# Routed experts in four sets of widths, one chosen on the chip, and two other edits to the second phase

## The chip, the cores and the metric

The kernel runs on one core of one Trainium2 chip. The metric is the device time of one execution in microseconds (us). The core has five engines that work side by side, each with its own queue of instructions which it takes in order: TensorE (PE; its weight loads are listed as PEld), VectorE (DVE), ScalarE (ACT), GpSimd (POOL) and SyncE (SP), which here issues most of the DMA transfers. An engine whose next instruction waits for another engine's result, or for a transfer, lets everything behind it in its queue wait too. "L272" means line 272 of the kernel's source.

## The reference

There are 8192 tokens of 512 numbers. They are normalised (`xn`) and go two ways: through a recurrent layer (`s`), and through a feed-forward part made of one shared expert for all tokens and 32 routed experts, of which each token takes the one with its largest gate logit (`g`). The end is `x + s * silu(g)`.

```python
scores = jax.nn.sigmoid(topk_val)[:, None]
xs = x * scores
tokens_per_expert = jnp.zeros((E,), jnp.int32).at[topk_ids].add(1)
order = jnp.argsort(topk_ids)
sorted_x = xs[order]
g = _grouped_mm(sorted_x, routed_gate_w, tokens_per_expert)
u = _grouped_mm(sorted_x, routed_up_w, tokens_per_expert)
d = _grouped_mm(jax.nn.silu(g) * u, routed_down_w, tokens_per_expert)
...
x = x + s * g
```

The gate and up weights of a routed expert are 512 by 1024 and the down weights 1024 by 512, all in fp32, so an expert brings 6 MB of weights. How many tokens an expert gets depends on the data. With the inputs of the reference, the counts, worked out from its own gate and sorted, are 343, 331, 311, 306, 306, 301, 298, 274, 272, 270, 266, 265, 265, 263, 258, 251, 250, 243, 243, 242, 237, 234, 233, 231, 228, 224, 222, 218, 217, 202, 197, 191.

## The kernel before

**Phase one** is dense. It runs over 16 chunks of 512 tokens; a written-out order of slots, 140 to a chunk (`SC`), says at which slot which step is issued (`at(slot, step)`, main loop L1429). TensorE does the input projections in `plain` and `multiply` (L701 to L802) and, as a filler between them, the output projections in `project_out` (L1030 to L1084). A unit of `project_out` is half a chunk's output: seven products P1, P2, P6, P5, P7, P3, P4 of 16 matmuls each (the line of the matmul is L1055), accumulated in two PSUM banks, `chain` and `side`. P2, P5 and P3 share `side`, so P5 cannot begin before VectorE has taken P2's result out of it (L1067: `o[0] = ps + part["a1"]`). The weights of a product come from DRAM into one of the tiles `wP`, or `far` for some of the last ones, loaded ahead by SP (L985, L988).

**The dispatch** (class `Dispatch`, L1086 to L1341) turns the gate's choices into a table: it counts the tokens of each expert, sorts the experts by count (`places`, L1156), gives the k-th largest the k-th entry of the constant list `WIDTHS`, works out each token's place (`slots`, L1240), enters the tokens into a table in DRAM by 64 scattered DMAs on POOL (`enter`, L1301), and reads it back as `idx` (`ids`, L1329). For the gathers a second form is wanted, `fours`: `numbers` (L1332) issues eight DMAs from POOL that bring the table into SBUF in two halves, and three slots later VectorE converts each half (L1338):

```python
at(now + 3, lambda: nc.vector.tensor_scalar(
    pools["fours"][:, 2 * half : 2 * half + 2, :], f, float(NA), piece[:, 0:1],
```

These steps are issued in the slots behind the last chunk, amid the last unit of `project_out`.

**Phase two** runs over the 32 experts, largest first (L1495 to L1523). Each is a `Chunk` (L170 to L363) of a fixed number of columns W, its entry of `WIDTHS` (376 down to 224, 8832 in sum); columns beyond its tokens are empty work. In `compute` (L253), eight steps j each do 4 matmuls into `e_g`, 4 into `e_u` (both L272) and, one step late, 4 into the four PSUM tiles `acc` (L261). A program matmul appears as two MATMUL records in the trace, since the numbers are fp32, so an expert is 192 records of width W. ACT (L277) and DVE (L279, L280) make `e_h` of `e_g` and `e_u`. The other steps hang between the eight: the transposes of the next expert's tokens (DVE, L248) at steps 5 to 7, the gathers of the tokens of the expert after next (POOL, L213) at step 2, the gather of the rest of the rows (POOL, L223) at step 6, the loads of the weights two experts ahead (SP, L193) at steps 1 and 7, and the finish of the expert before (DVE, ACT, and a scatter to the output on POOL, L360). Seven weight slots lie in the pools `wa` (four) and `wb` (three), each slot a tile of its own. The gathered tokens have `2 * CT` buffers (CT is 3), the rest rows `CT + 2`.

**Behind phase two** a loop (L1528 to L1556) would take experts whose count exceeds their width: it reads the number of such chunks, `nov`, into a register on each engine (L1529). With these inputs it runs zero times.

Of the kernel before, what the change touches and what calls it, by code (L numbers as in the profile page):

```python
# [17 lines left out]
P = 128  # L18
# [5 lines left out]
CT = C // P  # L24

WIDTHS = (
    376, 352, 336, 320, 320, 312, 304, 296, 296, 296, 288, 280, 280, 280, 272, 272,
    272, 264, 264, 264, 256, 256, 248, 248, 248, 240, 240, 240, 232, 232, 224, 224,
)
EPS = 1e-5  # L30


@with_exitstack
def tile_kernel(
# [14 lines left out]
    rdown_w: bass.AP,  # L49
    out: bass.AP,  # L50
):

# [27 lines left out]
    nc = tc.nc  # L80
# [20 lines left out]
    const = ctx.enter_context(tc.tile_pool(name="const", bufs=1))  # L101
# [6 lines left out]
    def work(name):  # L108
        return pools["work"].tile([P, 512], FP, tag="w", name=name)

    pools = {}
# [4 lines left out]
    ones = const.tile([P, P], FP, name="ones")  # L116
# [22 lines left out]
    iot = iota("iot", NIO, 1, 0)  # L139
    thr = iota("thr", KOV, C, 0)  # L140
    descp = iota("descp", 1, 0, E, -1)
    wid = const.tile([P, E], FP, name="wid")

    def widths(first, last):
        for e in range(first, last):
            nc.vector.memset(wid[:, e : e + 1], float(WIDTHS[e]))

    tok = iota("tok", NTILE, P, 0, cm=1)
    mhalf = const.tile([P, NT], FP, name="mhalf")
# [9 lines left out]
    ovexp = const.tile([P, MAXOV], I32, name="ovexp")  # L159
    nov = const.tile([P, 1], I32, name="nov")  # L160
    eid = const.tile([P, E], I32, name="eid")

    def expert(where):
        e = nc.values_load(
            where, engines=[ET.SP], min_val=0, max_val=E - 1,
            skip_runtime_bounds_check_because="the numbers of experts, or a count of them, clamped",
        )
        return [w[bass.ds(e, 1)].rearrange("o a b -> (o a) b") for w in (rgate_w, rup_w, rdown_w)]

    class Chunk:  # L170
# [133 lines left out]
        def store(self):  # L304

            nb = -(-self.width // BL)
            self.y = ydram[next(yturn) % len(ydram)]
            rows = self.y.rearrange("(b c) (a d) -> a c b d", c=BL, a=NA)
            for a in range(NA):
                nc.sync.dma_start(  # L310
                    out=rows[a, :, :nb, :],
                    in_=self.yT[a * BL : (a + 1) * BL, :nb].rearrange("p b m r -> p b (m r)"),
                )
# [51 lines left out]

    accs = []
    ydram = [dram.tile([C, H], FP, name=f"ydram{q}") for q in range(3)]
    yturn = iter(range(E))
    NW = 7
    turn = iter(range(3 * E))  # L370

    def alloc_w(shape, name):
        i = next(turn) % NW
        return pools["wa" if i < 4 else "wb"].tile(shape, FP, tag=f"w{i}", name=name)

    def alloc2(shape, tag, name):
        bufs = {"xs": 2 * CT, "xsT": 2, "sig": 2, "h": 3, "y": 3, "s": 2, "yT": 2, "rest": CT + 2}
        pool = pools["in" if tag in ("xs", "xsT") else "by"]
        return pool.tile(shape, FP, tag=tag, name=name, bufs=bufs[tag])

    chunks = [
        Chunk(
            alloc2, alloc_w, f"e{e}",
            lambda t, e=e: pools["idx"][:, e * CT + t : e * CT + t + 1],
            lambda t, b, e=e: pools["fours"][:, b, e * CT + t : e * CT + t + 1],
            WIDTHS[e], lambda e=e: expert(eid[0:1, e : e + 1]), e == 0, e == E - 1,
        )
        for e in range(E)
    ]

# [43 lines left out]
    class Prep:  # L434
# [127 lines left out]
        def plan(self, g):  # L562

            g += 50 if self.c == 1 else 0
            for t in range(NT):
                at(g + 2 + 2 * t, self.load, t)
                at(g + 16 + 2 * t, self.stats, t)
                at(g + 32 + 2 * t, self.normal, t)
                at(g + 35 + 2 * t, self.store, t)
                at(g + 43 + 2 * t, self.pieces, t)  # L570
                at(g + 50 + 2 * t, self.turn, t)
                late = 70 if self.c == NCHUNK - 1 else 0
                at(g + 72 + late + 2 * t, self.again, t)
# [512 lines left out]
    class Dispatch:  # L1086
# [69 lines left out]
        def places(self):  # L1156
# [26 lines left out]
            yield  # L1183
            at_pos = row("at_pos")
            nc.vector.tensor_scalar(at_pos, iot[:E, :E], pos[:, 0:1], None, ALU.is_equal)
            nc.vector.tensor_tensor(gt, at_pos, wid[:E, :], ALU.mult)
            we = total(gt, "we")
            rest = col("left")
            nc.vector.tensor_tensor(rest, cnt, we, ALU.subtract)
            ov = row("ov", KOV)  # L1190
# [141 lines left out]
        def numbers(self, half):  # L1332

            f = self.big([P, 2, NCOL], f"number{half}")
            rows = self.table.rearrange("(b c) q -> c b q", c=BL)[:, 2 * half : 2 * half + 2, :]
            for a in range(NA):
                nc.gpsimd.dma_start(out=f[a * BL : (a + 1) * BL, :, :], in_=rows)
            at(now + 3, lambda: nc.vector.tensor_scalar(  # L1338
                pools["fours"][:, 2 * half : 2 * half + 2, :], f, float(NA), piece[:, 0:1],
                ALU.mult, ALU.add,  # L1340
            ))  # L1341
# [50 lines left out]
    def table():  # L1392
        for part in (d.ranks(NCHUNK // GC - 1), d.places(), d.slots()):
            yield from part
        first = now + 3
        end = first + (21 * NTILE) // 10
        for i in range(NTILE):
            at(first + (21 * i) // 10, d.enter, i)
        at(end + 4, d.collect)
        for which in range(4):  # L1400
            at(end + 13 + which, d.merge, which)
        end = max(end + 17, END + 1)
        at(end, d.ids)
        at(end + 1, chunks[0].gather_in)
        for half in range(2):
            at(end + 2, d.numbers, half)
# [22 lines left out]
    for now in range(END):  # L1429
# [15 lines left out]
    pools["idx"] = ix.tile([P, NCOL], I32, name="idx")  # L1445
    pools["fours"] = ix.tile([P, NA, NCOL], I32, name="fours")
    c2 = ExitStack()
    pools["wa"] = c2.enter_context(
        tc.tile_pool(name="wa", bufs=1, side="right", reuse_waits="tile")
    )  # L1450
    pools["in"] = c2.enter_context(
        tc.tile_pool(name="in2", bufs=2, side="right", reuse_waits="tile")
    )
    ps_w = ctx.enter_context(
        tc.tile_pool(name="ps_w", bufs=4, space=PSUM, side="right", reuse_waits="tile")
    )
# [4 lines left out]
    k = 0  # L1461
# [29 lines left out]
    with ExitStack() as c3:  # L1491
        pools["wb"] = c3.enter_context(tc.tile_pool(name="wb", bufs=1, reuse_waits="tile"))
        pools["by"] = c3.enter_context(tc.tile_pool(name="by", bufs=2, reuse_waits="tile"))
        chunks[1].gather_in()
        for e, chunk in enumerate(chunks):  # L1495
            between = {j: [] for j in range(NI)}
            if e:
                before = chunks[e - 1]
                between[0].append(before.store)
                between[1].append(before.fetch)  # L1500
                for t in range(CT):
                    between[1 + t].append(lambda t=t: before.bias(t))
                    between[3 + t].append(lambda t=t: before.sums(t))
                    between[4 + t].append(lambda t=t: before.finish(t))
            if e == 0:
                for j, tag in enumerate("gud"):
                    between[j].append(lambda tag=tag: chunks[1].weight(tag))
            if e + 2 < E:
                between[3 if e == 0 else 1].append(lambda: chunks[e + 2].weight("g"))
                between[2].append(chunks[e + 2].gather_in)  # L1510
            if e + 1 < E:
                for t in range(CT):
                    between[5 + t].append(lambda t=t: chunks[e + 1].transpose(t))
            between[6].append(chunk.gather_rest)
            if e + 2 < E:
                between[7] += [lambda q=q: chunks[e + 2].weight(q) for q in "ud"]
            if e == E - 1:
                for t in range(CT):
                    between[7].append(lambda t=t: chunk.bias(t))
            chunk.compute(between)  # L1520
        for t in range(CT):
            for step in (chunks[-1].sums, chunks[-1].finish):
                step(t)  # L1523
    order.close()
    c2.close()

# [62 lines left out]
```

## Time and profile before

| | us |
|---|---|
| median of three runs | 4239.5 (4238.96 to 4239.67) |
| the profiled execution | 4237.99 |
| its span | 4236.3 |
| TensorE busy | 4198.9 (99% of the span) |
| weight loads busy | 3527.2 (83%) |
| VectorE / ScalarE / GpSimd busy | 2083.9 / 1978.0 / 1105.3 |
| granted clock of TensorE | 0.997 |

The span is the time from the first to the last recorded instruction; the execution's own time is 1.7 us longer, and the median of the runs is 1.5 us above the profiled one. Matmuls are pipelined: successive records overlap, and the distance from one start to the next, not the listed duration of one, is what a matmul costs on the path. In the chain of waits (the work that ended last, followed back to what released each step) the pieces are given by that distance. Idle time of an engine that isn't the bottleneck costs nothing.

### The profile page before, as it was taken

The numbers are of one execution on the slowest core, as the hardware profiler recorded it, in microseconds if no ns is written. First come the engines' busy times: TensorE is split into PE (matmuls) and PEld (weight loads), VectorE is DVE, ScalarE is ACT, GpSimd is POOL, SyncE is SP. The second block draws the span as 40 slices with busy tenths as digits, with TensorE's granted clock in tenths as the row PEclk, the third lists the DMA queues.
The fourth block names the chain that finished last, engine by engine and source line by source line (L and its number), as shares of the span: only waits on it lengthen the run. The fifth ranks groups of instructions, "written<-read, shape, count | busy, mean of one in ns | idle before, by whom it ended". The sixth has DMA issues, their size and how long they took to land.

```text
span 4236.3 us, 51931 instructions
## 1 busy us (share of the span) xinstructions
PE 4198.9 (99%) x18719; PEld 3527.2 (83%) x18719; DVE 2083.9 (49%) x3425; ACT 1978.0 (47%) x3577; POOL 1105.3 (26%) x1182
## 2 busy tenths in 40 slices
PE   9999999999999999999999999999999999999998
PEld 4688888888888888888888888866777788889998
DVE  5555555544554545555545456424444444544444
ACT  5676676666666766666767666501111111111110
POOL 3222122111221121212211225442232333323221
PEclk9999999999999999999999999999999999999999
DMA  8767666666676666766666656575666567677773
GB/s 277 244 214 231 207 216 216 210 223 206 213 226 216 217 213 203 231 202 216 222 210 220 214 177 205 179 267 181 211 227 226 205 236 242 222 253 242 243 263 113
DMA packets 506854, 925.61 MB, mean 218 GB/s; under 512 B 38397, under 2 KB 324509, under 8 KB 498402
## 3 DMA queue, kind: packets, MB, share of 16 engines
q1 hardware_dynamic: 478754, 831.89, 59.2%
q0 software_dynamic: 27840, 90.36, 6.4%
q8 instruction: 150, 2.46, 0.2%
q14 instruction: 110, 0.90, 0.1%
HBM read 805.27 MB, written 134.92 MB: 222 GB/s over the span
## 4 chain that ended last, share of the span: by engine, by line
PE 97%; DVE 1%; DMA 1%; issue 0%; ACT 0%; POOL 0%; SPq 0%; POOLq 0%; ACTq 0%
PE b L759 24%; PE u L1055 18%; PE c L759 12%; PE e_u L272 11%; PE e_g L272 11%; PE acc L261 11%; PE a L759 6%; PE b L710 3%; PE lgp L520 0%; DMA e_xs<-rec,idx 0%; PE lgt L530 0%; PE b L725 0%; DMA x<-in_L_attn_x_dram 0%; DMA e_rest<-rec,idx 0%; POOL s L1007 0%
## 5 line engine op out<-in xcount | busy, mean ns | idle before, releaser
L759 PE MATMUL b<-t,sums 128*128 128x256 f32 x2400 | 616.1, 379 | 1.2 <-DVE t L681 1.2
L1055 PE MATMUL u<-wP,s 128*128 128x256 f32 x2032 | 598.4, 380 | 6.1 <-issue 6.1
L277 ACT ACTIVATE e_sig<-e_g 128x280 f32<-128x280 f32 (+15 forms) x256 | 101.8, 398 | 931.8 <-PE e_g L272 931.6
L272 PE MATMUL e_u<-e_xsT,e_wu 128*128 128x296 f32 (+15 forms) x2048 | 518.0, 396 | 0.0
L272 PE MATMUL e_g<-e_xsT,e_wg 128*128 128x296 f32 (+15 forms) x2048 | 518.0, 396 | 0.0
L261 PE MATMUL acc<-e_h,e_wd 128*128 128x296 f32 (+15 forms) x2048 | 512.8, 396 | 0.0
L759 PEld LDWEIGHTS b<-t,sums 128*128 128x128 f32 x2400 | 454.8, 190 | 63.0 <-ACT a L773 1.3
L272 PEld LDWEIGHTS e_g<-e_xsT,e_wg 128*128 128x128 f32 x2048 | 389.1, 190 | 87.2
L272 PEld LDWEIGHTS e_u<-e_xsT,e_wu 128*128 128x128 f32 x2048 | 389.1, 190 | 87.1
L261 PEld LDWEIGHTS acc<-e_h,e_wd 128*128 128x128 f32 x2048 | 389.1, 190 | 87.1
L1055 PEld LDWEIGHTS u<-wP,s 128*128 128x128 f32 x2032 | 387.2, 191 | 61.1 <-issue 8.3
L279 DVE TENSOR_TENSOR e_sig<-e_sig,e_g 128x280 f32<-128x280 f32 (+15 forms) x256 | 113.1, 442 | 481.6 <-ACT e_sig L277 481.2
L213 POOL DMA_INDIRECT e_xs<-rec,fours x276 | 262.4, 951 | 178.2 <-DMA e_rest<-rec,idx 86.0
L759 PE MATMUL c<-xnT,sums 128*128 128x256 f32 x1200 | 308.0, 379 | 0.0
L759 PE MATMUL c<-t,sums 128*128 128x256 f32 x1200 | 308.0, 379 | 0.0
L759 PE MATMUL b<-xnT,nat 128*128 128x256 f32 x1200 | 308.0, 379 | 0.0
L759 PE MATMUL a<-xnT,nat 128*128 128x256 f32 x1200 | 308.0, 379 | 0.0
L759 PE MATMUL b<-t,nat 128*128 128x256 f32 x1200 | 308.0, 379 | 0.0
L360 POOL DMA_INDIRECT out_dram<-e_rest,idx x84 | 93.1, 1109 | 801.2 <-DVE e_rest L359 798.2
L759 PEld LDWEIGHTS b<-xnT,nat 128*128 128x128 f32 x1200 | 228.0, 190 | 31.4 <-issue 0.5
L759 PEld LDWEIGHTS a<-xnT,nat 128*128 128x128 f32 x1200 | 228.0, 190 | 31.0
L759 PEld LDWEIGHTS c<-t,sums 128*128 128x128 f32 x1200 | 228.0, 190 | 31.0
(243 smaller groups left out, 6381.2 us busy)
## 6 DMA issues: line engine op xcount, KB each, us to landing
sums<-sdram SPq DMA_DIRECT2D x300, 512.0 KB, 4.6
nat<-in_L_attn_W_dram SPq DMA_DIRECT2D x192, 512.0 KB, 4.6
e_wg<-L_ffn_routed_gate_w_dram SPq DMA_DIRECT2D x32, 2048.0 KB, 8.4
e_wu<-n_L_ffn_routed_up_w_dram SPq DMA_DIRECT2D x32, 2048.0 KB, 12.7
e_wd<-L_ffn_routed_down_w_dram SPq DMA_DIRECT2D x32, 2048.0 KB, 19.0
wP<-tdram SPq DMA_DIRECT2D x127, 512.0 KB, 3.5
nat<-L_ffn_shared_gate_w_dram SPq DMA_DIRECT2D x64, 512.0 KB, 4.9
nat<-n_L_ffn_shared_up_w_dram SPq DMA_DIRECT2D x64, 512.0 KB, 4.3
```

The costliest lines, as they stand in the source:

```text
L213: nc.gpsimd.indirect_dma_start(out=r[:, b, :], out_offset=None, in_=rec1.rearrange("n (a d) -> (n a) d", a=NA), in_offset=bass.IndirectOff ...
L261: nc.tensor.matmul(accs[m][:, :W], lhsT=wd[:, j, m * P : (m + 1) * P], rhs=h[:, :W], start=(j == 0), stop=(j == NI - 1),)
L272: nc.tensor.matmul(o[:, :W], lhsT=w[:, k, j * P : (j + 1) * P], rhs=xsT[:, k, :W], start=(k == 0), stop=(k == KH - 1),)
L277: nc.scalar.activation(sig[:, :W], g[:, :W], AF.Sigmoid)
L279: nc.vector.tensor_tensor(sig[:, :W], sig[:, :W], g[:, :W], ALU.mult)
L360: store = nc.gpsimd.indirect_dma_start(out=of[:, :], out_offset=bass.IndirectOffsetOnAxis(ap=col[:n, :], axis=0), in_=o, in_offset=None, b ...
L710: nc.tensor.matmul(ps[:, part], lhsT=natural[n][:, k, block * P : (block + 1) * P], rhs=xnTs[0][:, k, part], start=(k == 0), stop=(k == KH ...
L759: nc.tensor.matmul(ps, lhsT=lhs[:, k, :], rhs=rhs[:, k, :], start=(new and k == 0), stop=(k == KQ - 1),  skip_group_check=True,)
L1055: nc.tensor.matmul(ps[:, q, :], lhsT=lhs[:, q * P : (q + 1) * P], rhs=w[:, p, :],  start=(q == 0 and p == 0 and name in ("P1", "P2", "P5") ...
```

## The change

The list `WIDTHS` stays as the widest of four sets; three narrower ones are added (`NARROW`), with sums of 8628, 8664 and 8704 columns. In `places`, the count of each expert is compared with its width in all four sets. A matmul against ones (`over`) adds up, for each narrow set, how many experts exceed it; VectorE takes the first set that none exceeds, writes its number to `which_set`, and uses its widths for the table of places. By the counts above, the first set is exceeded by four experts (331 over 328, 306 over 304, 301 over 296, 298 over 292); in the second set none is, the closest by 6.

The code of phase two is written out four times, once for each set. Behind the memsets of `acc` every engine reads `which_set` into a register and branches: the first set's code, or else the second's, or else the third's, or else the widest's. Each engine skips the bodies that aren't chosen.

The seven weight slots become two tiles, one of four slots and one of three, that stay for all four bodies. The gathers move from step 2 to step 7 and have `CT` buffers in place of `2 * CT`; the rest rows have `CT + 1`. The conversion to `fours` is issued 26 slots behind the DMAs in place of 3, which puts it behind P3's eviction (L1078) and ahead of the memsets of `acc` in VectorE's queue. The tokens are entered every 1.9 slots in place of 2.1, and two steps of the last chunk (`again`, `scale`) are issued 14 slots later. In chunk 0, 96 more memsets write the widths of the narrow sets.

```diff
@@ NARROW, three lists of 32 widths, behind WIDTHS
+        352, 340, 320, 316, 312, 308, 304, 300, 292, 288, 288, 284, 280, 280, 276, 272,
+        268, 264, 260, 256, 256, 248, 244, 240, 236, 236, 232, 228, 224, 220, 220, 220,
...
     def alloc_w(shape, name):
-        i = next(turn) % NW
-        return pools["wa" if i < 4 else "wb"].tile(shape, FP, tag=f"w{i}", name=name)
+        i = turns["w"] % NW
+        turns["w"] += 1
+        return pools["wa"][:, i, :] if i < 4 else pools["wb"][:, i - 4, :]
...
-        bufs = {"xs": 2 * CT, "xsT": 2, "sig": 2, "h": 3, "y": 3, "s": 2, "yT": 2, "rest": CT + 2}
+        bufs = {"xs": CT, "xsT": 2, "sig": 2, "h": 3, "y": 3, "s": 2, "yT": 2, "rest": CT + 1}
...
-                late = 70 if self.c == NCHUNK - 1 else 0
+                late = 84 if self.c == NCHUNK - 1 else 0
...
-            nc.vector.tensor_tensor(gt, at_pos, wid[:E, :], ALU.mult)
-            we = total(gt, "we")
+            wes, over = row("wes", K + 1), row("over", K)
+            by_set = self.big([E, K + 1, E], "by_set")
+            nc.vector.tensor_tensor(
+                by_set, at_pos.unsqueeze(1).to_broadcast([E, K + 1, E]),
+                wid[:E, :].rearrange("p (k e) -> p k e", e=E), ALU.mult,
+            )
+            nc.vector.tensor_reduce(wes, by_set, AX.X, ALU.add)
+            nc.vector.tensor_scalar(over, wes[:, :K], cnt[:, 0:1], None, ALU.is_lt)
+            for _ in range(3):
+                yield
+            ps = work("over")
+            nc.tensor.matmul(ps[:, :K], lhsT=ones[:E, :], rhs=over, start=True, stop=True)
+            for _ in range(2):
+                yield
...
+            nc.vector.tensor_scalar(fit, ps[:, :K], 0.0, None, ALU.is_equal)
...
+            nc.vector.tensor_copy(which_set, first_set)
...
+            nc.vector.tensor_tensor(wes, wes, sel, ALU.mult)
+            we = total(wes, "we")
...
-            at(now + 3, lambda: nc.vector.tensor_scalar(
+            at(now + 26, lambda: nc.vector.tensor_scalar(
...
-            at(first + (21 * i) // 10, d.enter, i)
+            at(first + (19 * i) // 10, d.enter, i)
...
-                between[2].append(chunks[e + 2].gather_in)
+                between[7].append(chunks[e + 2].gather_in)
...
+        set_now = nc.values_load(
+            which_set[0:1, 0:1], min_val=0, max_val=K,
...
+        def second(k):
+            turns["w"], turns["y"] = begun, 0
+            chunks_ = first_chunks(SETS[k], "abcdefgh"[k])
+            chunks_[0].wt, chunks_[0].xsT = chunks[0].wt, chunks[0].xsT
+            with tc.tile_pool(name=f"by{k}", bufs=2, reuse_waits="tile") as pools["by"]:
+                experts(chunks_)
+
+        def choose_set(k):
+            if k == K:
+                second(k)
+                return
+            with tc.If(set_now == k) as cmp:
+                second(k)
+            with cmp.Else():
+                choose_set(k + 1)
+
+        choose_set(0)
```

More of the change, by code (lines that the diff above doesn't have):

```diff
@@ L28 @@
     272, 264, 264, 264, 256, 256, 248, 248, 248, 240, 240, 240, 232, 232, 224, 224,
+)
+NARROW = (
+    (
+        344, 328, 320, 308, 304, 296, 292, 288, 288, 284, 280, 280, 276, 272, 272, 268,
+        268, 264, 260, 260, 256, 252, 252, 248, 244, 244, 240, 236, 232, 228, 224, 220,
+    ),
+    (
+        352, 340, 320, 316, 312, 308, 304, 300, 292, 288, 288, 284, 280, 280, 276, 272,
+        268, 264, 260, 256, 256, 248, 244, 240, 236, 236, 232, 228, 224, 220, 220, 220,
+    ),
+    (
+        376, 352, 336, 324, 316, 308, 304, 296, 292, 288, 284, 280, 276, 272, 268, 264,
+        260, 260, 256, 252, 252, 248, 248, 244, 240, 236, 236, 236, 232, 228, 220, 220,
+    ),
 )
@@ L141, in tile_kernel @@
     descp = iota("descp", 1, 0, E, -1)
-    wid = const.tile([P, E], FP, name="wid")
+    K = len(NARROW)
+    SETS = NARROW + (WIDTHS,)
+    for widths_ in SETS:
+        assert len(widths_) == E and widths_[0] <= WIDTHS[0]
+    wid = const.tile([P, (K + 1) * E], FP, name="wid")
     def widths(first, last):
         for e in range(first, last):
-            nc.vector.memset(wid[:, e : e + 1], float(WIDTHS[e]))
+            for k in range(K + 1):
+                i = k * E + e
+                nc.vector.memset(wid[:, i : i + 1], float(SETS[k][e]))
     tok = iota("tok", NTILE, P, 0, cm=1)
@@ L161, in tile_kernel @@
     eid = const.tile([P, E], I32, name="eid")
+    which_set = const.tile([P, 1], I32, name="which_set")
     def expert(where):
@@ L306, in store @@
             nb = -(-self.width // BL)
-            self.y = ydram[next(yturn) % len(ydram)]
+            self.y = ydram[turns["y"] % len(ydram)]
+            turns["y"] += 1
             rows = self.y.rearrange("(b c) (a d) -> a c b d", c=BL, a=NA)
@@ L367, in tile_kernel, with first_chunks @@
     ydram = [dram.tile([C, H], FP, name=f"ydram{q}") for q in range(3)]
-    yturn = iter(range(E))
     NW = 7
-    turn = iter(range(3 * E))
+    turns = {"w": 0, "y": 0}
     def alloc_w(shape, name):
-        i = next(turn) % NW
-        return pools["wa" if i < 4 else "wb"].tile(shape, FP, tag=f"w{i}", name=name)
+        i = turns["w"] % NW
+        turns["w"] += 1
+        return pools["wa"][:, i, :] if i < 4 else pools["wb"][:, i - 4, :]
     def alloc2(shape, tag, name):
-        bufs = {"xs": 2 * CT, "xsT": 2, "sig": 2, "h": 3, "y": 3, "s": 2, "yT": 2, "rest": CT + 2}
[L378 to L389, printed above, removed]
+        if "by" not in pools:
+            return in0.tile(shape, FP, tag=tag, name=name, bufs={"xs": CT, "xsT": 1}[tag])
+        bufs = {"xs": CT, "xsT": 2, "sig": 2, "h": 3, "y": 3, "s": 2, "yT": 2, "rest": CT + 1}
+        return pools["by"].tile(shape, FP, tag=tag, name=name, bufs=bufs[tag])
+    def first_chunks(widths, name=""):
+        return [
+            Chunk(
+                alloc2, alloc_w, f"{name}e{e}",
+                lambda t, e=e: pools["idx"][:, e * CT + t : e * CT + t + 1],
+                lambda t, b, e=e: pools["fours"][:, b, e * CT + t : e * CT + t + 1],
+                widths[e], lambda e=e: expert(eid[0:1, e : e + 1]), e == 0, e == E - 1,
+            )
+            for e in range(E)
+        ]
+    chunks = first_chunks(WIDTHS)
     NP = DI // (2 * P)
@@ L1185, in places @@
             nc.vector.tensor_scalar(at_pos, iot[:E, :E], pos[:, 0:1], None, ALU.is_equal)
-            nc.vector.tensor_tensor(gt, at_pos, wid[:E, :], ALU.mult)
-            we = total(gt, "we")
+            wes, over = row("wes", K + 1), row("over", K)
[3 more added lines that the diff above has]
+                wid[:E, :].rearrange("p (k e) -> p k e", e=E), ALU.mult,
+            )
+            nc.vector.tensor_reduce(wes, by_set, AX.X, ALU.add)
[6 more added lines that the diff above has]
+                yield
+            fit = one.tile([P, K], FP, name="fit")
+            score = one.tile([P, K], FP, name="score")
+            first_set = one.tile([P, 1], FP, name="first_set")
+            nc.vector.tensor_scalar(fit, ps[:, :K], 0.0, None, ALU.is_equal)
+            nc.vector.tensor_scalar(score, iot[:, :K], -1.0, float(K), ALU.mult, ALU.add)
+            nc.vector.tensor_tensor(fit, fit, score, ALU.mult)
+            nc.vector.tensor_reduce(first_set, fit, AX.X, ALU.max)
+            nc.vector.tensor_scalar(first_set, first_set, -1.0, float(K), ALU.mult, ALU.add)
+            nc.vector.tensor_copy(which_set, first_set)
+            sel = row("sel", K + 1)
+            nc.vector.tensor_scalar(
+                sel, iot[:E, : K + 1], first_set[:E, 0:1], None, ALU.is_equal
+            )
+            nc.vector.tensor_tensor(wes, wes, sel, ALU.mult)
+            we = total(wes, "we")
             rest = col("left")
@@ L1395, in table @@
         first = now + 3
-        end = first + (21 * NTILE) // 10
+        end = first + (19 * NTILE) // 10
         for i in range(NTILE):
-            at(first + (21 * i) // 10, d.enter, i)
+            at(first + (19 * i) // 10, d.enter, i)
         at(end + 4, d.collect)
@@ L1447, in tile_kernel @@
     c2 = ExitStack()
[L1448 to L1453, printed above, removed]
+    wa = c2.enter_context(tc.tile_pool(name="wa", bufs=1, side="right", reuse_waits="tile"))
+    pools["wa"] = wa.tile([P, 4, KH * I], FP, name="wa")
+    in0 = c2.enter_context(tc.tile_pool(name="in0", bufs=1, side="right", reuse_waits="tile"))
     ps_w = ctx.enter_context(
@@ L1490, in tile_kernel, with experts @@
         accs.append(acc)
-    with ExitStack() as c3:
-        pools["wb"] = c3.enter_context(tc.tile_pool(name="wb", bufs=1, reuse_waits="tile"))
-        pools["by"] = c3.enter_context(tc.tile_pool(name="by", bufs=2, reuse_waits="tile"))
+    def experts(chunks):
         chunks[1].gather_in()
@@ L1523, in tile_kernel @@
                 step(t)
+    with ExitStack() as c3:
+        wb = c3.enter_context(tc.tile_pool(name="wb", bufs=1, reuse_waits="tile"))
+        pools["wb"] = wb.tile([P, 3, KH * I], FP, name="wb")
+        set_now = nc.values_load(
+            which_set[0:1, 0:1], min_val=0, max_val=K,
+            skip_runtime_bounds_check_because="K less a number from 0 to K",
+        )
+        begun = turns["w"]
+        def second(k):
[13 more added lines that the diff above has]
+        choose_set(0)
     order.close()
```

## The prediction, made before the changed kernel ran

> **What bounds the kernel now.** First the page: its head, the chain of waits by engine, and the groups of the experts' matmuls.
>
> ```profile
> span 4236.3 us, 51931 instructions
> ...
> PE 97%; DVE 1%; DMA 1%; issue 0%; ACT 0%; POOL 0%; SPq 0%; POOLq 0%; ACTq 0%
> ...
> L272 PE MATMUL e_u<-e_xsT,e_wu 128*128 128x296 f32 (+15 forms) x2048 | 518.0, 396 | 0.0
> L272 PE MATMUL e_g<-e_xsT,e_wg 128*128 128x296 f32 (+15 forms) x2048 | 518.0, 396 | 0.0
> L261 PE MATMUL acc<-e_h,e_wd 128*128 128x296 f32 (+15 forms) x2048 | 512.8, 396 | 0.0
> ```
>
> TensorE is the bound; its expert groups have no idle time before them, so a column left out there comes off the span. 3 x 2048 records over 32 experts are 192 each. Two pieces of the chain give the price of a column, at the widest and the narrowest expert, and the weight loads stand beside the second:
>
> ```profile
> 2842.54 5.05 PE acc L261 x16
> ```
> ```profile
> 4176.09 3.03 PE acc L261 x16
> ```
> ```profile
> 4195.41 1.51 PEld L272 LDWEIGHTS e_g<-e_xsT,e_wg 128*128 128x128 f32 x8
> ```
>
> 16 records take 5.05 us at W 376 and 3.03 at W 224: 315.6 and 189.4 ns each, 0.83 ns per column at both ends. The waits of TensorE come next; the one of more than a moment near the change is 6.1 us at L1055. Its place by the timelines of TensorE and VectorE, then the granted clock (the column before the last two) by stretches:
>
> ```profile
> 2759.65 3.62 PE L1055 MATMUL u<-wP,s 128*128 128x256 f32 x16
> 2769.33 5.83 PE L1055 MATMUL u<-wP,s 128*128 128x256 f32 x16 [6.06 <-issue]
> 2774.99 1.59 PE L240 MATMUL e_tp<-ident,e_xs 128*128 128x128 f32 x12
> 2776.42 3.63 PE L1055 MATMUL u<-wP,s 128*128 128x256 f32 x16
> 2779.89 3.62 PE L1055 MATMUL u<-far,s 128*128 128x256 f32 x16
> 2783.34 3.62 PE L1055 MATMUL u<-far,sh 128*128 128x256 f32 x16
> 2786.79 2.69 PE L272 MATMUL e_g<-e_xsT,e_wg 128*128 128x376 f32 x8
> ```
> ```profile
> 2762.33 1.40 DVE L1338 TENSOR_SCALAR fours<-number,piece 128x372 int32<-128x372 f32 x1 [7.12 <-DMA number<-table]
> 2766.87 0.41 DVE L1338 TENSOR_SCALAR fours<-number,piece 128x372 int32<-128x372 f32 x1 [3.15 <-DMA number<-table]
> 2767.20 1.42 DVE L1007 TENSOR_TENSOR s<-sh,s 128x256 f32<-128x256 f32 x4
> 2768.54 0.68 DVE L1067 TENSOR_TENSOR o<-u,a 128x512 f32<-128x512 f32 x1
> ```
> ```profile
> 2760.00:2770.00 10.00, 3.94 (x18) 3.15 (x17) 3.75 (x7) 0.58 (x1) 3.30 (x5) 0.84 1.03 396
> ```
>
> The rows from 2759.65 on are P6, P5, P7, P3 and P4 of the last unit, and the transposes of the first expert. P5 could start at 2763.1, 3.45 behind P6's start, but its bank is freed by L1067, which stands in VectorE's queue behind two conversions that wait for the table's DMAs. When P5 comes it takes 5.66 us to the next group instead of 3.45: the clock has fallen.
>
> **The change part by part.** The sum is made against the profiled execution (4237.99, span 4236.3) and carried to the median, 4239.5, which is 1.5 above it.
>
> *Widths.* The second set fits the counts, by 6 at the closest. 8832 - 8664 = 168 columns x 192 records x 0.83 ns = **-26.8 us**. Nothing between the records covers it, as TensorE has no idle time there. Bound on the other side: a weight load can be a floor. The narrowest measured expert has one load per 189 ns, the same as its matmul, so no row shows loads faster than that beside expert matmuls; three experts go to 220, at 186 ns. Were 189 the floor, 3 x 192 x 3.3 ns = 1.9 us would stay. The nearest row is of another shape: seven loads for `e_tb` took 0.81 us at the end, 116 ns each. I take no floor. Half the new widths are multiples of 4 and not of 8, which no row shows; I take the same slope.
>
> *Conversions.* Moved behind P3's eviction (L1078), they leave the queue ahead of L1067, and P5 starts at 2763.1 (its weights landed at 2761.3 by the semaphore records). It keeps the clock: 2766.6; transposes 1.43: 2768.0; P7: 2771.5. Late next are P3's weights, `far`, landed at 2772.75: a wait of 1.25. P3 to 2776.2, P4 to 2779.65, where the first expert starts instead of at 2786.79: **-7.1 us**. Ends: -8.4 without the wait for `far`, 0 if something else holds P5 or P7. The wait added moves to the conversions, which now find their data (landed by 2767) at about 2777; behind them in VectorE's queue are the memsets of `acc` (2.1 us, 2784.48 before), wanted by the first down product 9.5 us after the expert's start. The next expert's gathers, which read `fours`, stand on POOL behind L1074 in any case and began 4.6 us ahead of the first expert's start; their data is wanted at +38, so the 2 to 5 us they lose are covered.
>
> *Entry.* Each engine reads `which_set`, finds it is not 0, jumps over a body and falls through the second compare. The page shows no such jump, but the raw records of TensorE's end do: its read of `nov` took 0.49 us and the jump over the empty loop 3.87, with an instruction DMA of 16 KB inside. POOL, DVE, ACT and SP jumped there in 0.04 to 0.06, to near targets. Over a body of 3134 TensorE instructions the target is far. TensorE's sequencer runs ahead, though: the records of its queue pass 4.6 us before the matmuls they let through, some 18 matmuls, 3.9 us of P4 at 0.216 each. 0.6 + 3.87 + 0.3 = 4.8 against 3.9: **+1.0 us**. Ends: 0, and +8: a second fetch (3.87) when the target lies at the end of its block, and a fall of the clock as at P5 (+2.2). The jumps of the others are covered: SP's loads and POOL's gathers for the second expert have over 15 us, and VectorE, if it enters at +6, has 3.5 us to the first down product.
>
> The Trainium skill (Advanced Engine Details and Errata, Control Flow Timing) gives compare-and-branch as about 108 ns. By that the time is that of the cheap jumps below; the record of 3.87 disagrees, and it decides. What speaks against this change is the skill's Runtime: NRT & Kernel Launch, Instruction fetch mechanics: a taken branch out of the two pages at hand waits for its page; the trace agrees, with the 16 KB packet inside the jump.
>
> *Exit.* Behind the body each engine jumps over the other two. The end is POOL's: its last scatter was issued at 4223.94, then it waits for the landing, and the span ends 12.3 us later. A far jump of POOL, 3.2 to 3.9, lies partly beside the landing (2.8): **+1.5 us**, between 0 and +5.
>
> *Edits at nothing.* Gathers from step 2 to 7 with half the buffers: at W 272 the transposes began 31.6 us into the expert before, and the last landing, now 16 to 18 into it, still has over 12 us; the queue they are moved past is POOL's, where the gather of the rest (0.95 us each) goes ahead, a gain for it. Rest buffers: where landings of scatters were 3517.3 to 3527.2, the gathers went out at 3526.3 to 3529, so one buffer fewer still leaves one free (0 to +1). Two tiles of weights: every load waits for the same matmul as before: 0. The choice: TensorE comes to `over` at about 2512.3, VectorE has it at 2511.5; a dozen more small VectorE steps of 0.17 to 0.2 us lie ahead of `terms`, which has some 7 us (0 to +2). Entering: five slots later at the start and eight earlier at the end, and `idx` hangs on `END` in both, 0. `again` and `scale`, 14 slots later, are wanted by the gathers only: 0. 96 memsets at 0.06 us are beside solid TensorE: 0.
>
> Sum: -26.8 - 7.1 + 1.0 + 1.5 = -31.4; span 4204.9, and in the measure of the runs 4239.5 - 31.4 = **4208.1 us**.
>
> **The rivals.**
> - *Dear jumps.* Two fetches at the entry with the clock down, and all of POOL's jump at the end: +8 + 5 instead of +2.5, 4218.6. For it: two 16 KB packets near the recorded jump, and P5's fall of the clock. Against it: the second came after the jump had ended.
> - *Cheap jumps.* All targets near, 0.04 to 0.06 as on four engines before: nothing at entry and exit, 4205.6. Against it: the bodies are far longer than the loop.
> - *The stall stays.* P5 or P7 is held by a transfer, 4215.2. For it: the stretch 2760 to 2770 has the DMA at 1.03 of its share. Against it: all but `far` had landed.
> - *The choice isn't what it says.* The third set: 128 columns, -20.4 instead of -26.8, 4214.5. The widest: no gain but the stall's, 4234.9, within 0.2%. For it: only a wrong count; against it the 6 spare tokens.
> - *Slower: gathers come too late.* With one set of buffers, a gather can't start before the transposes one expert ahead have read its buffer. For it: POOL's gathers (L213) waited 86.0 us in all for `e_rest`, and landings took up to 13.4 us where 8.0 is the median. Against it: 86.0 over 31 experts is 2.8, and 5.4 more for the landing, together 8.2, under the 12 to spare. It ends the gain at 31.4 us in all, 1.05 at each of 30 experts, and is slower beyond 39.9, 1.33 at each. Landings 15 us later would cost 3 each: 4298.
>
> **How the numbers follow.** Forecast 0.61; cheap jumps 0.05; dear jumps 0.11; the stall stays 0.07; the third set 0.02, the widest 0.02; gathers late 0.06 (0.05 slower, 0.01 same); something unnamed that slows, 0.06 (0.02 each way). The time is the forecast's. Its low end is 4202: -8.4 for -7.1 and nothing for the jumps give 4204.3, and 2 are left for hidden waits. Its high end takes in the dear jumps and the stall that stays: 4220. 0.2%, 8.5 us, is about what a measurement of this kernel can tell from no change: below 4231.0 is faster, above 4248.0 slower. Faster: 0.61 + 0.05 + 0.11 + 0.07 + 0.02 + 0.02 = 0.88; same 0.02 + 0.01 + 0.02 = 0.05; slower 0.05 + 0.02 = 0.07.
>
> **What would show it.** Widths: 16 records at L286 in 4.73 us for the first expert (352) and 2.98 for the last (220), 8664 columns in all. Conversions: P5 directly behind P6 in 3.45, about 1.2 of wait at P3, first `e_g` near 2779.7. Entry: a gap of about 1 ahead of that `e_g`, no fall of the clock. Exit: the last scatter to the end in 13 to 16 us, not 12.3. I am wrong if VectorE's transposes wait for `e_xs`, if TensorE has idle time between experts, or if the first expert's records aren't 352 wide.

## The result, and the profile after

The changed kernel takes 4225.35 us in the median of seven runs (4223.93 to 4227.39), the kernel before 4239.67 (4238.96 to 4240.54). The ratio is 0.9966, with a 95% interval of 0.9956 to 0.9975. It is faster by 14.3 us where 31.4 were forecast, and lies 5 us above the range. The head of the page, then TensorE's waits in the experts and behind them and VectorE's for `be_y` (us in total, times, longest); last, of the kernel before, TensorE's waits at P5 and behind the experts and VectorE's for `e_y`:

```profile
span 4224.2 us, 52099 instructions
```
```profile
...
PE acc L286 <- DVE be_h L305: 7.2, 3, 3.4
PE be_tb L358 <- DVE be_yT L316: 4.7, 1, 4.7
...
```
```profile
DVE be_rest L365 <- DMA be_y<-ydram: 64.7, 22, 10.0
```
```profile
...
PE u L1055 <- issue: 6.1, 1, 6.1
...
PE e_tb L332 <- DVE e_yT L291: 0.5, 1, 0.5
```
```profile
DVE e_rest L339 <- DMA e_y<-ydram: 23.7, 19, 2.4
```

The stall of 6.1 at P5 is gone. New are three waits of TensorE inside the experts, where the kernel before had none, and the wait ahead of the last transposes is 4.7 instead of 0.5. The transition itself went much as written. TensorE's timeline, P6 to the first expert:

```profile
2760.39 3.62 PE L1085 MATMUL u<-wP,s 128*128 128x256 f32 x16
2764.98 3.69 PE L1085 MATMUL u<-wP,s 128*128 128x256 f32 x16 [0.97 <-POOL s L1037]
2768.51 1.59 PE L265 MATMUL e_tp<-ident,e_xs 128*128 128x128 f32 x12
2769.94 3.63 PE L1085 MATMUL u<-wP,s 128*128 128x256 f32 x16
2773.40 3.62 PE L1085 MATMUL u<-far,s 128*128 128x256 f32 x16
2776.86 3.62 PE L1085 MATMUL u<-far,sh 128*128 128x256 f32 x16
2781.14 2.63 PE L297 MATMUL be_g<-e_xsT,wa 128*128 128x352 f32 x8 [0.67 <-DVE acc L1545]
```

P5 comes 4.59 behind P6 instead of 9.68, at full clock (1.00 granted from 2764.98 to 2768.5). The first expert is 352 wide, so the second set was chosen, and it starts 5.65 earlier.

Cut at the start of the first expert and at the first of the last transposes (the line `be_tb`), the two profiled executions differ so:

| stretch | before, us | after, us | difference | forecast |
|---|---|---|---|---|
| up to the first expert | 2786.79 | 2781.14 | -5.65 | -7.1 + 1.0 |
| the 32 experts | 1428.48 | 1413.36 | -15.12 | -26.8 |
| last transposes to the end | 21.03 | 29.70 | +8.67 | +1.5 |

So 11.7 us are missing in the experts and 7.2 behind them; the first row misses by under half a us. The table goes by two executions: in the traces of three other kernels with the old widths, shown further down (124 rows, the conversions alone, the later gathers alone), the last stretch takes 22.2 to 22.7, so 1.2 to 1.6 of its 8.67 belong to the one execution before. In the experts the loss lies in three places: 3.55 at 3875, 1.37 at 3919 and 2.76 at 4142 beyond the usual distance of two records, with 3.1 of slow clock behind the first and the third (granted 0.50 from 3881.1 to 3883.2 and 0.51 from 4146.1 to 4149.5) and 0.2 at one more record, 11.0 together. All three are in narrow experts (240, 236 and 220 columns). The first of them, in the timelines of TensorE and VectorE:

```profile
3873.85 1.78 PE L297 MATMUL be_u<-be_xsT,wa 128*128 128x240 f32 x8
3879.03 2.72 PE L286 MATMUL acc<-be_h,wa 128*128 128x240 f32 x8 [3.39 <-DVE be_h L305]
```
```profile
3865.95 0.40 DVE L305 TENSOR_TENSOR be_h<-be_sig,be_u 128x240 f32<-128x240 f32 x1 [0.24 <-PE be_u L297]
3876.36 0.69 DVE L365 TENSOR_TENSOR be_rest<-be_y,be_rest 128x512 f32<-128x512 f32 x1 [10.01 <-DMA be_y<-ydram]
3878.06 0.40 DVE L304 TENSOR_TENSOR be_sig<-be_sig,be_g 128x240 f32<-128x240 f32 x1 [1.00 <-ACT be_sig L302]
3878.57 0.40 DVE L305 TENSOR_TENSOR be_h<-be_sig,be_u 128x240 f32<-128x240 f32 x1
```

VectorE, in order, stands for 10 us at the sum of the expert before (L365), which wants `be_y`; the next `be_h` is behind it, and TensorE waits for that. `be_y` is the result of the expert before, which SP writes to DRAM in four pieces and reads back. SP's queue of the changed kernel around it, and then that of the kernel before at the same expert:

```profile
3844.81 0.36 SPq L218 DMA_DIRECT2D wa<-n_L_ffn_routed_up_w_dram  x1
3846.45 0.38 SPq L218 DMA_DIRECT2D wb<-L_ffn_routed_down_w_dram  x1
3850.23 16.15 SPq L336 DMA_DIRECT2D ydram<-be_yT  x4
3873.62 0.74 SPq L345 DMA_DIRECT2D be_y<-ydram  x2
```
```profile
3865.65 0.34 SPq L193 DMA_DIRECT2D e_wu<-n_L_ffn_routed_up_w_dram  x1
3867.32 0.38 SPq L193 DMA_DIRECT2D e_wd<-L_ffn_routed_down_w_dram  x1
3871.15 7.89 SPq L310 DMA_DIRECT2D ydram<-e_yT  x4
3885.20 0.85 SPq L319 DMA_DIRECT2D e_y<-ydram  x2
```

From the first piece to the fetch it is 23.4 us instead of 14.1. In the kernel before this stretch is 16.6 in the median of the 31 experts and at most 18.4; after, its three longest, 23.4, 20.9 and 20.7, lie just ahead of the three waits. The share of the DMA engines that is busy shows where the pieces stand, in 40 slices (tenths) of 3849.5 to 3874 after and of 3870.5 to 3895 before, then the last microseconds ahead of the fetch after (the last columns are the clock, the share of the 16 DMA engines that is busy, and GB/s):

```profile
DMA  9969997949899999999999999932592222221000
```
```profile
DMA  8898989989999999999994100389995899999720
```
```profile
3868.00:3872.00 4.00, 4.00 (x21) 3.77 (x20) 0.00 (x0) 0.00 (x0) 0.00 (x0) 1.00 0.25 82
```

Before, nearly all engines are busy until the pieces have landed. After, most run dry at 3866, are busy once more at 3867, and from 3868 to 3872 a quarter of them works on. By the sizes of the packets these are first rows of the down weights (2 KB), then the pieces of y (512 bytes). From 3847 to 3850, too, rows of 6 KB, the size of the rest rows, hold 0.26 of the engines, and the weights have the others. The last expert, where no weights are loaded any more, shows what is slow by itself. Its second tile has 220 - 128 = 92 rows (before: 96). VectorE's timeline after, and the stretches in which the rest rows of that tile are gathered, after and then before:

```profile
4198.41 0.69 DVE L374 TENSOR_TENSOR be_rest<-be_rest,b2b 92x512 f32<-92x512 f32 x1 [4.24 <-DMA be_rest<-rec,idx]
```
```profile
4193.50:4197.50 4.00, 1.28 (x8) 0.96 (x6) 0.67 (x1) 0.69 (x2) 0.00 (x0) 0.98 0.25 106
```
```profile
4210.00:4213.00 3.00, 3.00 (x17) 3.00 (x16) 0.94 (x3) 0.36 (x1) 0.00 (x0) 1.00 0.96 342
```

For four us the share is 0.25, a quarter of the DMA engines: 92 rows are moved by 4 of 16. That gather took 9.98 us from issue to landing, and the transposes waited for it by way of VectorE. 92 = 4 x 23, and the other late gather, 22.7 us long, is that of expert 22, 244 wide, with 116 = 4 x 29 rows. The second of the three waits isn't explained by this alone: it is for the y of expert 23, whose tiles have 128 and 112 rows. It comes one expert behind the first wait, and goes together with it below; that the first delay carries over is inferred.

### The profile page after: what moved, and what is told of

It is laid out like the page before. It is cut to its first block, busy times and chain, and to the rows that moved or that the text cites. A ratio compares the mean times of both kernels' runs of the same rounds, so it can differ in the third digit from the quotient of the medians.

```text
span 4224.2 us, 52099 instructions
## 1 busy us (share of the span) xinstructions
PE 4175.7 (99%) x18721; PEld 3529.3 (84%) x18721; DVE 2078.5 (49%) x3525; ACT 1975.8 (47%) x3576; POOL 1105.2 (26%) x1175
## 5 line engine op out<-in xcount | busy, mean ns | idle before, releaser
L302 ACT ACTIVATE be_sig<-be_g 128x220 f32<-128x220 f32 (+25 forms) x256 | 100.4, 393 | 890.0 <-PE be_g L297 886.4
L304 DVE TENSOR_TENSOR be_sig<-be_sig,be_g 128x220 f32<-128x220 f32 (+25 forms) x256 | 111.2, 434 | 443.9 <-ACT be_sig L302 439.5
L238 POOL DMA_INDIRECT be_xs<-rec,fours x271 | 259.4, 957 | 210.1 <-DMA be_rest<-rec,idx 112.0
L386 POOL DMA_INDIRECT out_dram<-be_rest,idx x83 | 92.9, 1119 | 765.4 <-DVE be_rest L385 749.5
L286 PE MATMUL acc<-be_h,wa 128*128 128x352 f32 (+17 forms) x1152 | 286.8, 395 | 6.0 <-DVE be_h L305 6.0
L297 PE MATMUL be_g<-be_xsT,wa 128*128 128x220 f32 (+16 forms) x1152 | 283.3, 389 | 0.0
L297 PE MATMUL be_u<-be_xsT,wa 128*128 128x288 f32 (+15 forms) x1152 | 281.6, 387 | 0.0
L286 PEld LDWEIGHTS acc<-be_h,wa 128*128 128x128 f32 x1152 | 219.2, 191 | 52.9 <-DVE be_h L305 7.1
L789 PEld LDWEIGHTS c<-xnT,sums 128*128 128x128 f32 x1200 | 228.2, 190 | 30.8
L789 PEld LDWEIGHTS b<-t,nat 128*128 128x128 f32 x1200 | 228.2, 190 | 30.8
```

Of the source, the lines that this page charges most:

```text
L238: nc.gpsimd.indirect_dma_start(out=r[:, b, :], out_offset=None, in_=rec1.rearrange("n (a d) -> (n a) d", a=NA), in_offset=bass.IndirectOff ...
L286: nc.tensor.matmul(accs[m][:, :W], lhsT=wd[:, j, m * P : (m + 1) * P], rhs=h[:, :W], start=(j == 0), stop=(j == NI - 1),)
L297: nc.tensor.matmul(o[:, :W], lhsT=w[:, k, j * P : (j + 1) * P], rhs=xsT[:, k, :W], start=(k == 0), stop=(k == KH - 1),)
L302: nc.scalar.activation(sig[:, :W], g[:, :W], AF.Sigmoid)
L304: nc.vector.tensor_tensor(sig[:, :W], sig[:, :W], g[:, :W], ALU.mult)
L386: store = nc.gpsimd.indirect_dma_start(out=of[:, :], out_offset=bass.IndirectOffsetOnAxis(ap=col[:n, :], axis=0), in_=o, in_offset=None, b ...
```

## The experiments

**Theory.** A gather or scatter of n rows on POOL is spread over as many DMA engines as the largest number up to 16 that divides n. The second set brings 116 rows at expert 22 and 92 at the last three; those land late and hold up what follows on the same engines. **Rivals:** the shorter experts leave the DMA too little time whatever the rows are; the branches or the fourfold code slow the queues; the later gathers do it.

**Four widths raised by 4**, so that no tile has 92 or 116 rows:

```diff
-        268, 264, 260, 256, 256, 248, 244, 240, 236, 236, 232, 228, 224, 220, 220, 220,
+        268, 264, 260, 256, 256, 248, 248, 240, 236, 236, 232, 228, 224, 224, 224, 224,
```

> The changed kernel with four widths of its second set raised by 4: 244 to 248 and three times 220 to 224, so that the last tiles have 120 and 96 rows instead of 116 and 92. Theory (a gather or scatter over 116 or 92 rows is spread over 4 of the 16 DMA engines only, and what queues behind it makes TensorE wait): the three waits at L286 (3.55, 1.4 and 2.8 us, with the slow clock behind them 11.0 in all) go, the wait of the last transposes (4.5) goes, the last scatter lands 2.2 earlier; 16 columns more cost 16 x 192 x 0.83 ns = 2.5. Together 15.2 less: 4210. Rival (shorter experts leave the DMA too little time whatever the rows are, or the fourfold code slows the queues): the waits stay, 2.5 more, 4228.

Measured: 4210.99 us (before 4240.25), with no wait of TensorE left in the experts. Compared with the changed kernel, more columns made it 14 us faster.

**All widths kept, the rows rounded up to a multiple of 16** in the gather of the rest rows and in the scatter of the results. The added rows are empty places of the table.

```diff
+    def even(n):
+        return -(-n // 16) * 16
...
-                    out=r[:n, :], out_offset=None, in_=rec2[:, :],
+                    out=r[: even(n), :], out_offset=None, in_=rec2[:, :],
...
-                out=of[:, :], out_offset=bass.IndirectOffsetOnAxis(ap=col[:n, :], axis=0),
-                in_=o, in_offset=None, bounds_check=N - 1, oob_is_err=False,
+                out=of[:, :], out_offset=bass.IndirectOffsetOnAxis(ap=col[: even(n), :], axis=0),
+                in_=r[: even(n), H : 2 * H], in_offset=None, bounds_check=N - 1, oob_is_err=False,
```

> The changed kernel with all its widths, but the gather of the rest rows and the scatter of the results go over the rows rounded up to a multiple of 16 (96 for 92, 128 for 116). No column is added. Theory of the 4 engines: 11.0 + 4.5 + 2.2 less, 4207.6, near the time that was predicted; rest gathers of the last tiles land in 15 us or less. Rival (the shorter experts as such): no change or a little slower, 4225 to 4227, since more rows are moved.

Measured: 4208.05 us, ratio 0.9925 (0.9909 to 0.9942), 17.3 below the changed kernel and 2.9 below the one with four raised widths. TensorE waits nowhere in the experts, and the 32 experts take 1401.69 us instead of 1428.48 before: 26.8 less, the forecast of the widths. SP's queue at the place shown above:

```profile
3849.57 6.19 SPq L339 DMA_DIRECT2D ydram<-be_yT  x4
3862.08 0.74 SPq L348 DMA_DIRECT2D be_y<-ydram  x2
```

The pieces of y are issued in 6.19 instead of 16.15, and the fetch follows the first by 12.5 instead of 23.4, with the same experts, code and branches. In this trace the 512-byte packets of y end at 3861, with no stretch at a quarter of the engines ahead of that. SP's fetch of y itself still goes over 92 and 116 rows here (`fetch` is as it was), so it isn't what delays.

**One body, no branch** (`choose_set(0)` replaced by `second(1)`, the read of `which_set` left out):

> The changed kernel with its second set written out alone: no read of the set's number, no branch, one body instead of four. Theory: the three waits and the late end stay as they are; the gap at the entry (0.8 us) and the scatter slowed by instruction fetches at the exit (1.7 us) go: 4222.5. Rival (the fourfold code or the branches bring the waits): most of the missing 17 us comes back, 4210 or less.

Measured: 4223.94 us. Three waits are there as before, at 3876, 3958 and 4143 (2.9, 0.5 and 3.9 beyond the usual distance), the first and the last of them in the same experts, so neither branch nor fourfold code makes them. The time is 1.4 below the changed kernel's, where 2.8 were expected.

**One gather of the kernel before over 124 rows, and over 128.** The widths are the old ones.

```diff
+    def rows(chunk, t, n):
+        return 124 if chunk.name == "e22" and t == 1 else n
...
-                    out=r[:n, :], out_offset=None, in_=rec2[:, :],
+                    out=r[: rows(self, t, n), :], out_offset=None, in_=rec2[:, :],
```

> The kernel before, with one gather changed: the rest rows of the second tile of expert 22 (width 248) are 124 instead of 120, four rows more than are used. Widths, branches and everything else as before. Theory (124 = 4 x 31 goes over 4 engines, 120 over 15): that gather lands about 20 us after its issue, expert 23's step waits as in the changed kernel, 3 to 6 us more: 4243 to 4246. Rival (rows don't matter, the shorter experts do): 4239.5, no wait.

> Control of the kernel before with 124 rows: the same gather of expert 22 now over 128 rows instead of 120. Theory (128 rows lie on 16 engines): as before, 4239 to 4240.5, expert 23 as long as expert 24. Rival (any more rows at this place bring the wait): 4245 as with 124.

Measured: 4245.24 us with 124 (before 4240.25; ratio 1.0013, 1.0003 to 1.0022), and with 128 4258.69 on a chip on which the kernel before takes 4258.9. SP's queue with 124, then with 128:

```profile
3871.69 14.86 SPq L315 DMA_DIRECT2D ydram<-e_yT  x4
3893.03 0.85 SPq L324 DMA_DIRECT2D e_y<-ydram  x2
```
```profile
3891.98 1.81 SPq L315 DMA_DIRECT2D ydram<-e_yT  x4
3899.92 0.85 SPq L324 DMA_DIRECT2D e_y<-ydram  x2
```

Four rows that nobody uses cost 5.0 us by the medians in a kernel that has none of the other edits; eight cost nothing. It needs neither a shorter expert nor a branch. The trace with 124 rows is that of the fastest of its ten executions (4241.25, the slowest 4248.2): there the gather lands some 22 us after its issue, VectorE waits 7.8 for `e_y`, and TensorE in expert 23 only 0.9, so the 5 us aren't seen in it as one wait.

**The rows measured by themselves.** Twelve gathers behind the last scatter of the kernel before, one after the other.

```diff
+        for n in (128, 112, 96, 120, 100, 84, 124, 116, 92, 98, 97, 128):
+            nc.gpsimd.indirect_dma_start(
+                out=last.rest[0][:n, :], out_offset=None, in_=rec2[:, :],
+                in_offset=bass.IndirectOffsetOnAxis(ap=last.cols(0)[:n, :], axis=0),
+            )
```

> The kernel before, with twelve gathers of rest rows added behind its last scatter, each into the same tile and so one after the other, with 128, 112, 96, 120, 100, 84, 124, 116, 92, 98, 97 and 128 rows; nothing uses them. With no other traffic the time from issue to landing should tell on how many DMA engines the rows lie. Theory: the largest number up to 16 that divides the rows: 16, 16, 16, 15, 10, 14, 4, 4, 4, 14, 1, 16. The rows are moved in some 0.24 us each on an engine, so 116 and 124 rows take 7 us and 97 take 23, on top of some 2.5 of start; all others 4 to 5. Rival (only multiples of 8 are spread over all engines): 100, 84 and 98 are as slow as 92 and 116, and 97 no worse.

Of this kernel there is one execution. POOL's timeline, from 96 rows on (96, 120, 100, 84, 124, 116, 92, 98, 97, 128); the wait in brackets is for the gather before. Then the stretches in the middle of the gathers of 116 and of 97 rows:

```profile
4237.59 0.91 POOL L1526 DMA_INDIRECT e_rest<-rec,idx  x1 [4.35 <-DMA e_rest<-rec,idx]
4242.77 0.97 POOL L1526 DMA_INDIRECT e_rest<-rec,idx  x1 [4.27 <-DMA e_rest<-rec,idx]
4249.36 0.99 POOL L1526 DMA_INDIRECT e_rest<-rec,idx  x1 [5.62 <-DMA e_rest<-rec,idx]
4255.83 0.93 POOL L1526 DMA_INDIRECT e_rest<-rec,idx  x1 [5.48 <-DMA e_rest<-rec,idx]
4261.10 1.30 POOL L1526 DMA_INDIRECT e_rest<-rec,idx  x1 [4.35 <-DMA e_rest<-rec,idx]
4273.43 1.25 POOL L1526 DMA_INDIRECT e_rest<-rec,idx  x1 [11.03 <-DMA e_rest<-rec,idx]
4283.92 1.17 POOL L1526 DMA_INDIRECT e_rest<-rec,idx  x1 [9.24 <-DMA e_rest<-rec,idx]
4293.18 0.95 POOL L1526 DMA_INDIRECT e_rest<-rec,idx  x1 [8.09 <-DMA e_rest<-rec,idx]
4298.49 2.15 POOL L1526 DMA_INDIRECT e_rest<-rec,idx  x1 [4.36 <-DMA e_rest<-rec,idx]
4325.59 0.95 POOL L1526 DMA_INDIRECT e_rest<-rec,idx  x1 [24.95 <-DMA e_rest<-rec,idx]
```
```profile
4277.00:4281.00 4.00, 0.00 (x0) 0.00 (x0) 0.00 (x0) 0.00 (x0) 0.00 (x0) 0.50 0.25 103
4305.00:4323.00 18.00, 0.00 (x0) 0.00 (x0) 0.00 (x0) 0.00 (x0) 0.00 (x0) 0.50 0.06 26
```

From issue to landing: 4.9 us with 96 or 128 rows, 5.0 with 84 and 98, 6.3 with 120, 6.2 with 100, but 12.0, 10.2 and 9.0 with 124, 116 and 92, and 26.8 with 97. A quarter of the engines is busy with 116 rows and a sixteenth with 97. By the packet records, the packets under way at one time are 4 in the median with 124, 116 and 92 rows, 1 with 97, 10 with 100, 13 with 84 and 98, and 14.5 to 16 with 96, 112, 120 and 128. 98 = 14 x 7 is fast, 97, a prime, is on one engine. The Trainium skill (DMA: Bandwidth & Descriptors, Why a DMA increments its semaphore by 16 and not by 1) gives this as the rule: the largest number up to 16 that divides the slowest dimension on both sides, which here is the rows. The shares of 0.25 and 0.06 and the counts agree with it. The rival that only multiples of 8 are well spread falls with 84, 98 and 100. The spread isn't all: 120 rows on 15 engines were expected in 4 to 5 us and take 6.3; their packets take 0.42 us in the mean, those of the last 128 rows 0.31, and why is open.

**The gathers alone rounded**, the scatters left at 92 and 116 rows, and both rounded once more beside it:

> The changed kernel with only the gathers of the rest rows rounded up to a multiple of 16; the scatters of the results keep 92 and 116 rows. Theory (the gathers make the waits, since the loads of the weights and the copies of y queue behind them; the scatters run beside little else): the three waits and that of the last transposes go, the last scatter over 92 rows still lands 2.2 late: 4210 to 4211. Rival (the scatters do the harm): 4220 or more.

> Only the gathers rounded, once more, beside the last. Theory: the scatters over 92 and 116 rows cost 2 to 3 us against the kernel with both rounded, of it 2.2 in the last landing. Rival (they also make the copies of y late): 5 or more.

> The changed kernel with rounded gathers and scatters once more, to stand beside the next kernel on one chip. Theory: as before in its share of the kernel before on the same chip, 0.9925 or, where that one waits for weights, less.

Measured, on two other chips: 4216.26 us (before 4258.9), and side by side 4217.78 with the gathers alone and 4219.14 with both (before 4259.27; ratios 0.9904, 0.9887 to 0.9921, and 0.9905, 0.9889 to 0.9922). With the gathers rounded, rounding the scatters as well brings nothing more: the 2 to 3 us that I put on them don't show, and from the last scatter to the end both take 13.9. So the 17.3 of the first chips are put down to the gathers; the changed kernel itself was not run on these two. The expected 4210 to 4211 can't be held against 4216.26, since on these chips the kernel before is some 19 us slower. No trace of it was kept from there; in that of the control with 128 rows the experts take 18.8 longer than in the trace before, 15 of it in the first expert. Here some waits of TensorE in the experts stay with rounded rows too: 8.1 us in eight places in the kernel with both rounded, from 256 columns down. They aren't the waits of the first chips: from 3690 to 4130 VectorE waits for `be_y` 12.4 us in this trace and 23.6 in the one without them, and a packet of 6 KB takes 0.23 us in the median on both. Whether the narrower experts bring them is not shown, so on these chips that rival is open.

**The conversions alone** (`at(now + 3` to `at(now + 26` in the kernel before), and **the gathers at step 7 with fewer buffers alone**:

> The kernel before with one edit: the two conversions to the table's second form are issued 26 slots behind their DMAs instead of 3. Theory: the whole gain of the conversions, without entry or exit: 7.1 less, 4233. Rival (something else holds P5 or P7): 4240, no change.

> The kernel before with one edit: the gathers at step 7 instead of 2 with half the buffers, and the rest rows with one buffer fewer. Theory: costs nothing, 4239 to 4241, since POOL comes to these gathers behind the gather of the rest rows in either order. Rival (late gathers bring part of the waits): 4243 or more.

Measured: 4232.25 us and 4239.56, before 4239.66. The conversions bring 7.4 where 7.1 were forecast; the later gathers cost nothing (ratio 1.000, 0.999 to 1.001).

**Rounded rows without branches:**

> The changed kernel with rounded rows, its second set written out alone, without the read of the set's number and the branches. Theory: against the same kernel with branches (4208.05) the entry gives back 0.7 and the exit 0.3 to 1.3: 4206 to 4207. Rival (dear jumps): 4203 or less. Rival (free jumps): 4208.

Measured: 4206.75 us. Against 4208.05 with branches, entry and exit cost about 1.3 together (2.5 forecast; the two were measured at different times and on different chips, with the kernel before at 4240.25 and 4239.66, so half a us either way is open). Against 4232.25 with the conversions alone, side by side, the widths and the other edits bring 25.5 where 26.8 were forecast.

## Why the prediction was wrong

- **The mechanism that was forecast holds.** With the rows rounded the kernel stands at 4208.05, and 4208.1 was predicted. That the two agree to 0.1 is luck: by the times the conversions bring 7.4 (forecast 7.1), the widths 25.5 (26.8), and the jumps cost 1.3 (2.5), misses that cancel. In the traces the experts alone are 26.8 shorter, as forecast. (The 0.83 ns of a column is the slope between the two widths; 315.6 / 376 and 189.4 / 224 are 0.84 and 0.85.)
- **The step that failed** is the term for the widths. It prices a column on TensorE, with "Nothing between the records covers it, as TensorE has no idle time there", and goes on: "Half the new widths are multiples of 4 and not of 8, which no row shows; I take the same slope." The slope held. What the term leaves out is the other thing a width sets, the number of rows in the last tile of the gathers and scatters. That cost was put at nothing, without a reason and without a bound, though the kernel before has only tiles of 8 to 128 rows in steps of 8, all of which divide well (120 over 15 engines, 104 over 13). The runs showed 17.3 us in its place, the whole miss: 11.0 in the experts, 4.9 at the last transposes, the rest in the last scatter. Only the 0.06 for something unnamed that slows had room for it.
- **The list of edits at nothing** named the gathers for their step and their buffers, which indeed cost nothing. The rival "gathers come too late" looked at the right queue, POOL's, and at other gathers: the transposes never waited for `be_xs`. The gathers of the rest rows were late and with them the copies of y, which stopped VectorE and by it TensorE, at 3 experts and not at 30.
- **Entry.** TensorE's read took 0.49 and its jump 3.91 in the raw records, as put (0.49 and 3.87), and the gap ahead of the first expert is 0.83 beyond the usual distance (1.0 was forecast; with one body it is nothing, 3.45 from P4 to the first expert). The other four engines' jumps were covered; VectorE's first step came 4.6 behind the expert's start.
- **P3's weights** were to be late next, by 1.25. In this trace P5 waited 1.0 for POOL's sums instead; in the kernel with one body P3 waits 1.2 for `far`, and with the conversions alone P5 waits 1.15 and P3 1.0. The size was right or short by one such wait, and the place varies.
- **Exit.** A far jump of POOL was put at 1.5. Its compare takes 0.04 and the next instruction follows 4.2 later, when the last landing (5.0) is not yet over: it hides behind the slow scatter. With 96 rows the last scatter lands 3.75 after its issue with branches (3.47 with the raised widths) and 2.77 without, so there up to 1.0 of the exit shows. The sign that was given, 13 to 16 us from the last scatter to the end, came true with 14.7, but for another reason. Of the 8.7 us lost behind the experts 4.2 is the wait for the 92 rows, 0.7 the slow clock of the transposes behind it (granted 0.50, before 1.00) and 2.2 the scatter over 92 rows (5.01 from issue to landing, 2.77 before; 4.94 with one body, so it isn't the branches). The last 1.7 is the first scatter, 4.92 instead of 3.20. That is not the change: in the kernel before with the twelve gathers added behind it, it takes 4.81, and with the conversions or the later gathers alone 4.48 and 4.74, so the one execution before is the odd one.
- **What is not settled.** That the loads of weights and the pieces of y end on as many engines as the gather has is seen in the share of 0.25 and the sizes of the packets; the records don't number the engines, so that they are the same four is inferred. 116 rows on 4 engines occupy those by some 5 us longer (29 rows of 0.23 us each, the median packet of 6 KB, instead of 8), while y came 9 later, and the issues on SP took longer as well; how the rest comes about is open.

## What to carry to other kernels

A width that is cut to save matmul time also sets the rows of every gather, scatter and copy that follows from it. Look at the divisors of the last tile's rows: 92, 116 and 124 go over four DMA engines, 97 over one, and rounding the rows up to a multiple of 16 cost nothing that showed here. When an edit sits off the bounding engine, ask which in-order queue connects it back; here one late copy stopped VectorE, and VectorE stopped TensorE.

## What was not expected of the hardware

The 4 and 1 busy engines of 16 at 116 and 97 rows, with 10.2 and 26.8 us where 128 rows take 4.9. The issue of four pieces of y on SP itself took 16.15 us when the transfers ahead were late, where the kernel before has 1.8 to 11.7 over its 31 experts, 9.8 in the median. And the chips differ: the same kernel before takes 4240 on some and 4259 on others; why TensorE waits in the first expert there was not followed up.
